# One GpSimd queue, one VectorE queue, one ScalarE queue: moving the side work of an attention pass to other places in its unit

## The chip, the cores and the metric

The kernel runs on one core of one Trainium2 chip. The metric is the device time of one execution in microseconds (us), the median of three runs. Everything is 32-bit float.

## The reference, cut to what matters

The program applies two layers to an input of 8 images, 32 by 32 positions, 512 channels. The first layer is group norm, self-attention with 8 heads and a residual. The second layer, to which the change belongs, is a deformable attention over the first layer's output `x`, read as 4 images:

```python
x_ln = layernorm(x, ln_g, ln_b);  q = x_ln_flat @ wq + bq
o = gelu(depthwise_conv_7x7_stride2(q_img, dw_w) + dw_b)      # 49 taps a channel
offsets = conv_1x1(o, pw_w)                                   # 2 numbers a point
grid = (refs + tanh(offsets) + 1) * ...                       # 16 x 16 points
interp = bilinear(x, grid)                                    # 4 corner rows a point, weighted
k = v = interp @ wv + bv
attn = softmax((q @ mq_w) @ (k @ mk_w).T) per head;  msa = attn @ (v @ mv_w) @ mo_w
z = msa + x
out = gelu(layernorm(z) @ mlp_w + mlp_b) + z
```

In the kernel an "image" is one eighth of the data: 1024 tokens, 256 sampled points.

## The kernel before, in words

The kernel has two passes. The first (lines 396 to 810) does the first layer, and beside it the depthwise convolution of images 0 to 5. The second (from line 813) does the rest of the second layer, and is what the change touches.

**Units.** The second pass is 64 units, `n` = 0 to 63, made by `unit_steps`. A unit is a pair of heads of half an image, so an image has 8 units; the place of a unit in its image, n mod 8, is called its position, p0 to p7, below. A unit consists of scores (TensorE, `sc`), negative row maxima (VectorE, two `nmax` reductions of 128 x 1024 from PSUM), exponentials (ScalarE, `e`: eight activations, each with an accumulator read), two block transposes (VectorE, `sq`), each followed by two DMAs on SyncE's queue that finish the transpose (`sq_d`, `et`), reciprocals of the sums (`rs`), the product with the values one unit later (TensorE, `av`) and its scaling (VectorE, `attH`).

**Back steps.** With each unit one 128-token tile of the half-image before it goes through `back_steps`: `joined` (projection `wo`, then on VectorE `z`, its statistics, and the inverse deviation `mv`, whose power is taken by GpSimd), `norm` (VectorE, `zn`), `turned` (TensorE transposes `zn`, ScalarE copies them to `zT`), and in the next unit `mlp` (`wm`) and `biased` (VectorE, `res`). For every second tile ScalarE applies the GELU to two tiles (`gelu`), which takes one table load ahead of it and one after it to go back to the exponential; GpSimd adds `z` and stores (`end`), and adds a bias row to the next two residual tiles (`add`, `xr`). These last three fall into even units.

**Convolution.** The images 6 and 7 are convolved in the second pass by `conv_steps`, in two lanes. Lane 0 is VectorE alone (one `scalar_tensor_tensor` a tap, tile `chunk`). In lane 1 ScalarE multiplies into one of two `parts` buffers, and GpSimd adds it to `chunk`: a tap therefore waits until the addition two taps before it is done. A lane takes a chunk of 128 channels, 49 taps, after filling its padded plane (`fill` on TensorE, `fill_end` on VectorE).

**Points.** For the images 1 to 7 `point_steps` does, with `b` the image: `conv_load`, `conv_gelu` (ScalarE, the GELU table again), `offsets` (TensorE, then a tanh on ScalarE, then two transposes into a PSUM tile), `targets` (VectorE: `corners`, some twenty tiny instructions that end in the row indices `ii`), and for each half of the points `gather` (four indirect DMAs issued by GpSimd, one a corner, into the four `row` buffers) and `sample` (VectorE, four weighted additions of 128 x 512). The sampled rows are projected to keys and values ahead of the image's first unit (`key_step`, `value_step`).

**Order.** There is no scheduler: `at(place, step)` enters a step under a number, the steps are emitted in the order of these numbers, and `InOrder` keeps each engine's instructions in the order in which they are emitted. The number's whole part is the unit. So the places in the diff are orders in queues, not times. The places around the change, all within unit n:

```python
at(n, scores)                                   # sc, nmax x2, e x8
at(n + 0.02, lambda: att.moved(u, 0))           # first transpose
at(n + 0.04, lambda: att.moved(u, 1))           # second transpose
(n + 0.05, n + 0.13)                            # joined (z ... power on GpSimd), norm (zn)
at(n + 0.06, lambda: query_step(*divmod(n + 1, NHP)))
at(n + 1.1, lambda: att.product(u)); at(n + 1.2, scale)      # of unit n, so 0.1 and 0.2 of the next
ends = (n + 0.6, n + 1.03, n + 1.035)           # turned, mlp, biased
(gelu, 1.72), (end, 2.24)                       # of an odd tile's unit: 0.72 of an odd, 0.24 of an even one
(pair - 1.6, pair - 0.5)                        # fetch, add: `add` at 0.5 of an even unit
```

Of the kernel before, what the change touches and what calls it, by code (L numbers as in the profile page):

```python
# [9 lines left out]
F32 = mybir.dt.float32  # L10
I32 = mybir.dt.int32
AF = mybir.ActivationFunctionType
ALU = mybir.AluOpType
# [4 lines left out]
P = 128  # L18
# [11 lines left out]
NHP = NH // 2  # L30
# [210 lines left out]
def attention_then_deformable_attention(  # L241
# [30 lines left out]
    nc = tc.nc  # L272
# [17 lines left out]
    def mm_tile():  # L290
        return ps_mm.tile([P, QB], F32, tag="mm", name="mm")
# [65 lines left out]
    def at(place, step):  # L357
        due.append((place, len(due), step))
# [37 lines left out]
    with ExitStack() as l0:  # L396
# [3 lines left out]
        nc = InOrder(tc)  # L400
# [366 lines left out]
        for b in range(B):  # L767
# [20 lines left out]
            for hp in range(NHP):  # L788
                for qt in range(NT):
                    n = first + hp * NT + qt  # L790
                    if n % per == 0 and b > 0:
                        last, attT = attT, {}
# [10 lines left out]
                        at=qt % NQT,  # L803
# [9 lines left out]
    with ExitStack() as l1:  # L813
        nc = tc.nc


        def pool(name, bufs=1):
            return l1.enter_context(tc.tile_pool(name=name, bufs=bufs, reuse_waits="tile"))

        first, raw, late, late2, cv, cvhat, wp = (  # L820
            pool(n) for n in ("first", "raw", "late", "late2", "cv", "cvhat", "w2")
        )
        work = pool("work1", 2)
        nc = InOrder(tc)
# [30 lines left out]
        refs = cv.tile([P, 2, 2], F32, tag="refs", name="refs")  # L855
# [58 lines left out]
        chat, room = {}, {}  # L914

        def conv_fetch(b, cb):
            chat[b, cb] = cvhat.tile([P, NT, P], F32, tag="hat", name="hat", bufs=2)
            nc.sync.dma_start(chat[b, cb], hat_d[b][:, :, ts(cb, P)])

        def conv_load(b):  # L920
            room[b, "o"] = cv.tile([P, NC, NS], F32, tag="o", name="o")
            nc.sync.dma_start(room[b, "o"], o_d[b][:, :, :])

        def fill(b, cb, par):
            hat = chat[b, cb]
            room["ps"] = project(lambda c: hat[:, par * NC + c, :], lambda c: wq_r[:, c, :])

        def fill_end(lane, par):
            conv_pad(pads[lane], room["ps"], bq_row, par)
# [10 lines left out]
        def conv_gelu(b):  # L940
            o = room[b, "o"]
            for cb in range(NC):
                nc.scalar.activation(o[:, cb, :], o[:, cb, :], AF.Gelu, bias=dwb[:, cb : cb + 1])

        def offsets(b):
            o = room[b, "o"]
            ps = mm_tile()
            for cb in range(NC):
                nc.tensor.matmul(
                    ps[0:2, 0:NS], lhsT=pww[:, cb, :], rhs=o[:, cb, :],  # L950
                    start=(cb == 0), stop=(cb == NC - 1),
                )
            th = cv.tile([2, NS], F32, tag="th", name="th")
            nc.scalar.activation(th, ps[0:2, 0:NS], AF.Tanh)
            room["th"] = mm_tile()[:, 0:4]
            for h in range(2):
                nc.tensor.transpose(room["th"][:, ts(h, 2)], th[:, ts(h, P)], ident[0:2, 0:2])

        def targets(b):
            room[b, "ii"], room[b, "wt"] = corners(room["th"])  # L960

        def gather(b, h):
            for k in range(4):
                row = room["row", k] = cv.tile([P, C], F32, tag="row", name="row", bufs=4)
                nc.gpsimd.indirect_dma_start(
                    out=row,
                    out_offset=None,
                    in_=mid[b][:, :],
                    in_offset=bass.IndirectOffsetOnAxis(ap=room[b, "ii"][:, k, h : h + 1], axis=0),
                )  # L970
# [14 lines left out]
        def points(b):  # L985
            conv_load(b)
            conv_gelu(b)
            offsets(b)
            targets(b)
            for h in range(2):  # L990
                gather(b, h)
                sample(b, h)

        def corners(th):

            vt = nc.vector

            def small(name, dt=F32):
                return cv.tile([P, 4], dt, tag=name, name=name)

            co = small("co")
            vt.tensor_tensor(co, th, refs.rearrange("p h o -> p (h o)"), ALU.add)
            vt.tensor_scalar(co, co, 1.0, G / 2.0, ALU.add, ALU.mult)
            vt.tensor_scalar(co, co, 1.0, 0.5 * (W - 1), ALU.add, ALU.mult)
            ci = small("ci", I32)
            vt.tensor_copy(ci, co)
            cf = small("cf")
            vt.tensor_copy(cf, ci)
            up = small("up")
            vt.tensor_tensor(up, cf, co, ALU.is_gt)  # L1010
            c2 = cv.tile([P, 2, 4], F32, tag="c2", name="c2")
            vt.tensor_tensor(c2[:, 0, :], cf, up, ALU.subtract)
            vt.tensor_scalar(c2[:, 1, :], c2[:, 0, :], 1.0, None, ALU.add)
            w2 = cv.tile([P, 2, 4], F32, tag="w2", name="w2")
            vt.tensor_tensor(w2[:, 1, :], co, c2[:, 0, :], ALU.subtract)
            vt.tensor_scalar(w2[:, 0, :], w2[:, 1, :], -1.0, 1.0, ALU.mult, ALU.add)
            cl = cv.tile([P, 2, 4], F32, tag="cl", name="cl")
            vt.tensor_scalar(cl, c2, 0.0, float(W - 1), ALU.max, ALU.min)
            inside = cv.tile([P, 2, 4], F32, tag="inside", name="inside")
            vt.tensor_tensor(inside, cl, c2, ALU.is_equal)  # L1020
            vt.tensor_tensor(w2, w2, inside, ALU.mult)
            cl4 = cl.rearrange("p a (h o) -> p a h o", o=2)
            w4 = w2.rearrange("p a (h o) -> p a h o", o=2)
            wt = cv.tile([P, 4, 2], F32, tag="wt", name="wt")
            fi = cv.tile([P, 4, 2], F32, tag="fi", name="fi")
            for k in range(4):
                ax, ay = k % 2, k // 2
                vt.tensor_tensor(wt[:, k, :], w4[:, ax, :, 1], w4[:, ay, :, 0], ALU.mult)
                vt.scalar_tensor_tensor(
                    fi[:, k, :], cl4[:, ay, :, 0], float(W), cl4[:, ax, :, 1], ALU.mult, ALU.add  # L1030
                )
            ii = cv.tile([P, 4, 2], I32, tag="ii", name="ii")
            vt.tensor_copy(ii, fi)
            return ii, wt
# [144 lines left out]
        def conv_steps():  # L1179
            for lane, chunks in enumerate(((0, 3, 6), (1, 2, 4, 5, 7))):  # L1180
                free = 0.5 + lane
                for k in chunks:
                    b, cb = EARLY + k // NC, k % NC
                    first = next(n for n in range(60) if n + 0.49 > free)
                    fills = [first + 0.49, first + 0.55]
                    at(fills[0] - 1.8, lambda b=b, cb=cb: conv_fetch(b, cb))
                    for par, place in enumerate(fills):
                        at(place, lambda b=b, cb=cb, par=par: fill(b, cb, par))
                        at(place + 0.02, lambda lane=lane, par=par: fill_end(lane, par))
                    unit = int(fills[1]) + 1  # L1190
                    i = 0
                    while i < KS * KS:
                        points = unit % (2 * NHP) in range(NHP, NHP + 3)
                        count = 7 if lane else 3 if points else 5
                        for j in range(count):
                            if i == KS * KS:
                                break
                            place = 0.25 + 0.01 * j if not lane else 0.045 + 0.001 * j if j < 4 else 0.65 + 0.01 * j
                            at(unit + place, lambda b=b, cb=cb, i=i, lane=lane: tap(b, cb, i, lane))
                            free = unit + place  # L1200
                            i += 1
                        unit += 1

        def point_steps(b):
            last = 2 * NHP * b - NHP
            at(last - 1.5, lambda: conv_load(b))
            at(last - 0.035, lambda: conv_gelu(b))
            at(last + 0.535, lambda: offsets(b))
            at(last + 0.75, lambda: targets(b))
            for h, (p0, p1) in enumerate(((0.8, 1.22), (1.23, 2.22))):  # L1210
                at(last + p0, lambda h=h: gather(b, h))
                at(last + p1, lambda h=h: sample(b, h))
            first = 2 * NHP * b
            for hp, place in enumerate((-0.82, -0.815, 0.185, 1.18)):
                at(first + place, lambda hp=hp: key_step(b, hp))
            for t, place in enumerate((-0.81, 0.18)):
                at(first + place, lambda t=t: value_step(b, t))
# [75 lines left out]
```

## Time and profile before

| what | value |
|---|---|
| median of 3 runs (lowest, highest) | 3526.83 us (3524.01, 3528.84) |
| the profiled execution: its time, its span | 3522.86 us, 3521.2 us |
| mean granted TensorE clock | 0.984 |
| busy in the span: TensorE, VectorE, ScalarE, GpSimd | 3388.6, 2534.7, 1809.8, 1536.3 us |
| the second pass: first scores, last scores | 2297.0 us, 3451.3 us after the span's start |
| from 2300 us on: TensorE waited for `zn` | 41.7 us in 16 waits |
| one image without a fill of lane 0 (units 16 to 23, 2583.70 to 2740.59) | 156.9 us |

The profiler records one execution. Times are in us from the span's start. Line numbers are of little use here: every recorded call passes through a helper, line 54, so instructions are told apart by their tiles, written out<-in. A timeline line has the start, the duration of a run of equal instructions, the engine, the operation, the count, and in brackets the engine's idle time before it and what ended that.

### The profile page before, as it was taken

To read this page: it belongs to the slowest core of one execution; us is meant where nothing else is said; L and a number is where in the kernel's file an instruction comes from. 1 tells how busy PE (TensorE), PEld (TensorE's weight loads), DVE (VectorE), ACT (ScalarE), POOL (GpSimd) and SP (SyncE) were. 2 spreads that over 40 slices of the span, in tenths; PEclk is the share of its full clock that TensorE was granted. 3 is DMA by queue.
4 is the path that set the end of the run, shared out by engine and by line. 5 is a ranking of instruction groups with operands and counts; after the bars stand their busy time and mean duration, and the time that the engine had idled before them with its cause. 6 is when DMAs were issued, how large, how long until landed. Compare 5 with 4: busy or idle time off the path is not lost.

```text
span 3521.2 us, 45344 instructions
## 1 busy us (share of the span) xinstructions
PE 3388.6 (96%) x14568; PEld 1679.5 (48%) x14568; DVE 2534.7 (72%) x3373; ACT 1809.8 (51%) x3919; POOL 1536.3 (44%) x1903
## 2 busy tenths in 40 slices
PE   7999999999999999999999998889998989899998
PEld 4544554554554554455455444534444444444443
DVE  4767778888888888788888875257777676665654
ACT  3443355566566566566567562245555455554442
POOL 1001226646636646655654653215445353532222
PEclk9999999999999999999999999899999999999999
DMA  4666667766766666767766667445656555565653
GB/s 145 171 159 176 193 170 195 211 160 184 219 164 186 207 169 185 204 174 194 203 174 175 202 177 208 136 157 194 198 175 196 171 181 178 179 199 189 222 184 123
DMA packets 446589, 641.65 MB, mean 182 GB/s; under 512 B 77104, under 2 KB 240944, under 8 KB 444304
## 3 DMA queue, kind: packets, MB, share of 16 engines
q1 hardware_dynamic: 415712, 536.67, 52.4%
q0 software_dynamic: 29488, 100.00, 9.5%
q8 instruction: 116, 1.90, 0.2%
q10 hardware_dynamic: 1152, 2.10, 0.2%
q14 instruction: 121, 0.99, 0.1%
HBM read 246.38 MB, written 123.73 MB: 105 GB/s over the span
## 4 chain that ended last, share of the span: by engine, by line
PE 81%; POOL 4%; ACT 4%; DVE 4%; issue 3%; DMA 2%; SPq 2%; POOLq 0%; ACTq 0%; DVEq 0%
PE mm L54 51%; PE sc L54 16%; PE av L54 15%; ACT e L54 2%; SPq L54 2%; POOL chunk L54 1%; POOL row L54 1%; DVE chunk L54 1%; ACT L54 1%; DVE nmax L54 1%; POOL oa L54 0%; DMA et<-sq_d 0%; DMA sq_d<-sq 0%; POOL rows L54 0%; POOL hat L54 0%
## 5 line engine op out<-in xcount | busy, mean ns | idle before, releaser
L54 ACT ACTIVATE e<-sc,nmax 128x1024 f32<-128x1024 f32 (+1 forms) x1024 | 802.9, 797 | 597.1 <-DVE nmax L54 595.8
L54 DVE TENSOR_REDUCE nmax<-sc 128x1 f32<-128x1024 f32 (+1 forms) x640 | 751.4, 1215 | 383.7 <-PE sc L54 382.7
L54 DVE STREAM_TRANSPOSE sq<-e 128x1024 f32<-128x1024 f32 x640 | 764.3, 1224 | 241.4 <-ACT e L54 218.2
L54 POOL TENSOR_TENSOR oa<-part_x,oa 128x256 f32<-128x256 f32 x852 | 632.2, 742 | 574.7 <-ACT part_x L54 530.3
L54 PE MATMUL sc<-k,q 64*128 64x512 f32 x2048 | 536.6, 619 | 17.1 <-ACT e L54 15.4
L54 ACT ACTIVATE part_x<-pad_x,dww_x 128x256 f32<-128x256 f32 x852 | 434.9, 541 | 222.9 <-POOL oa L54 221.3
L54 PE MATMUL av<-et,v 128*64 128x256 f32 x4096 | 503.5, 388 | 13.9 <-DMA et<-sq 13.0
L54 PE MATMUL mm<-xT,wqkv 128*128 128x512 f32 x1024 | 470.6, 604 | 3.1 <-issue 3.1
L54 PEld LDWEIGHTS av<-et,v 128*64 128x64 f32 x4096 | 275.3, 137 | 319.2 <-issue 161.2
L54 POOL TENSOR_TENSOR chunk<-parts,chunk 128x256 f32<-128x256 f32 x240 | 179.9, 749 | 384.3 <-ACT parts L54 369.2
L54 PEld LDWEIGHTS sc<-k,q 64*128 64x128 f32 x2048 | 186.5, 187 | 280.0 <-issue 190.7
L54 PEld LDWEIGHTS mm<-xT,wqkv 128*128 128x128 f32 x1024 | 187.1, 190 | 240.3 <-issue 234.9
L54 POOL TENSOR_TENSOR mv<-mv,minus_half 128x1 f32<-128x1 f32 x128 | 77.3, 604 | 489.2 <-DVE mv L54 487.1
L54 PEld LDWEIGHTS mm<-wqkv,xT 128*128 128x128 f32 x2048 | 234.1, 192 | 25.7 <-issue 25.7
L54 PE MATMUL mm<-wqkv,xT 128*128 128x128 f32 x2048 | 244.8, 278 | 0.0
L54 PE MATMUL mm<-wm,zT 128*128 128x512 f32 x512 | 238.1, 608 | 1.3 <-ACT zT L54 1.0
L54 PE MATMUL mm<-w,attT 128*128 128x512 f32 x512 | 235.5, 604 | 1.7 <-DVE attT L54 1.7
L54 PE MATMUL mm<-wo,attH 128*128 128x512 f32 x512 | 230.8, 593 | 0.4
L54 PE MATMUL mm<-hat_h,wqq 128*128 128x512 f32 x512 | 230.7, 593 | 0.0
L54 DVE SCALAR_TENSOR_TENSOR od<-pad_x,dww_x,od 128x256 f32<-128x256 f32 x276 | 226.4, 820 | 5.5
L54 ACT ACTIVATION_READ_ACCUMULATOR e<-sc,nmax 128x1 f32 x1024 | 209.2, 204 | 0.0
L54 PE MATMUL mm<-w,hat_x 128*128 128x512 f32 x384 | 172.7, 600 | 0.0
(163 smaller groups left out, 3555.4 us busy)
## 6 DMA issues: line engine op xcount, KB each, us to landing
et<-sq SPq DMA_DIRECT2D x2048, 128.0 KB
sq_d<-sq SPq DMA_DIRECT2D x128, 512.0 KB
et<-sq_d SPq DMA_DIRECT2D x128, 512.0 KB
inv<-rs_d SPq DMA_DIRECT2D x256, 128.0 KB
hat_h<-hat_d SPq DMA_DIRECT2D x16, 1024.0 KB
xr<-mid SPq DMA_DIRECT2D x64, 256.0 KB
x<-in_x_dram POOLq DMA_DIRECT2D x60, 256.0 KB
out_dram<-res POOLq DMA_DIRECT2D x60, 256.0 KB
```

The source lines that it names most:

```text
L54: return self.tc.keep_in_program_order(op(*args, **kwargs))
```

## The change

Four things are moved; no arithmetic changes.

1. Lane 0's taps move from 0.25 of a unit (behind the scaling) to 0.002 (behind the maxima, ahead of the first transpose). They are 6 in a unit rather than 5, and 2 rather than 3 in the units of positions 4 to 6.
2. The first four of lane 1's seven taps in a unit move from 0.045 (ahead of `joined`) to 0.131 (behind `norm`). The other three stay at 0.69 to 0.71.
3. `point_steps` starts one unit earlier: GELU of the convolution at the end of p2, `offsets` at the end of p3. `corners` is split: its first addition, which reads the PSUM tile, is now `shift` at 0.75 of p3; the rest is at 0.011 of p4, behind the maxima and the taps.
4. The first half's `gather` goes from 0.8 of p4 to 0.14 of p4, its `sample` from 0.22 of p5 to 0.012 of p5; the second half's `gather` from 0.23 of p5 to 0.141 of p5, its `sample` from 0.22 of p6 to 0.012 of p6.

```diff
+        def shift(b):
+            co = room[b, "co"] = cv.tile([P, 4], F32, tag="co", name="co")
+            nc.vector.tensor_tensor(co, room["th"], refs.rearrange("p h o -> p (h o)"), ALU.add)
+
         def targets(b):
-            room[b, "ii"], room[b, "wt"] = corners(room["th"])
+            room[b, "ii"], room[b, "wt"] = corners(room[b, "co"])
...
-        def corners(th):
+        def corners(co):
...
-            co = small("co")
-            vt.tensor_tensor(co, th, refs.rearrange("p h o -> p (h o)"), ALU.add)
...
                         points = unit % (2 * NHP) in range(NHP, NHP + 3)
-                        count = 7 if lane else 3 if points else 5
+                        count = 7 if lane else 2 if points else 6
...
-                            place = 0.25 + 0.01 * j if not lane else 0.045 + 0.001 * j if j < 4 else 0.65 + 0.01 * j
+                            place = 0.002 + 0.001 * j if not lane else 0.131 + 0.001 * j if j < 4 else 0.65 + 0.01 * j
...
         def point_steps(b):
-            last = 2 * NHP * b - NHP
+            last = 2 * NHP * b - NHP - 1
             at(last - 1.5, lambda: conv_load(b))
             at(last - 0.035, lambda: conv_gelu(b))
             at(last + 0.535, lambda: offsets(b))
-            at(last + 0.75, lambda: targets(b))
-            for h, (p0, p1) in enumerate(((0.8, 1.22), (1.23, 2.22))):
+            at(last + 0.75, lambda: shift(b))
+            at(last + 1.011, lambda: targets(b))
+            for h, (p0, p1) in enumerate(((1.14, 2.012), (2.141, 3.012))):
                 at(last + p0, lambda h=h: gather(b, h))
                 at(last + p1, lambda h=h: sample(b, h))
```

Because lane 0 goes through its chunks faster, its second and third fills move from units 13 and 25 to units 12 and 24.

## Prediction

> **What bounds the kernel now.** I read the page first, then TensorE's waits from 2300 us on, then the timelines of one image, engine by engine.
>
> ```profile
> PE 3388.6 (96%) x14568; PEld 1679.5 (48%) x14568; DVE 2534.7 (72%) x3373; ACT 1809.8 (51%) x3919; POOL 1536.3 (44%) x1903
> ```
>
> TensorE is the bound; other engines matter only where TensorE waits for them. In the second pass that is one wait:
>
> ```profile
> PE mm L54 <- DVE zn L54: 41.7, 16, 4.9
> ```
>
> TensorE's timeline shows where: p4, p5 and p6 (units 20 to 22 here), the units of the points.
>
> ```profile
> 2675.07 0.65 PE L54 MATMUL mm<-ident,zn 128*128 128x128 f32 x4 [0.86 <-DVE zn L54]
> 2694.89 1.12 PE L54 MATMUL mm<-ident,zn 128*128 128x128 f32 x4 [4.51 <-DVE zn L54]
> 2716.38 0.66 PE L54 MATMUL mm<-ident,zn 128*128 128x128 f32 x4 [3.98 <-DVE zn L54]
> ```
>
> A unit without extra TensorE work takes 14.88 us (unit 19), and reaches the transposes of `zn` at 14.30. What makes `zn` late is a chain: exponentials, transposes, `z`, statistics, GpSimd's power, `zn`. In unit 16 the first transpose starts 8.40 us in, the power ends at 14.44: 6.0 us. With GpSimd free at once (unit 18: 8.38 and 14.14) it is 5.75, which I use. Then `zn` takes 0.55 us, or 1.48 beside a GpSimd addition. The exponentials are late where ScalarE hangs in a lane 1 tap behind GpSimd. GpSimd's timeline of an even unit (p0):
>
> ```profile
> 2597.58 0.56 POOL L54 TENSOR_TENSOR mv<-mv,minus_half 128x1 f32<-128x1 f32 x1
> 2598.09 1.28 POOL L54 TENSOR_TENSOR res<-res,z 128x512 f32<-128x512 f32 x1
> ...
> 2602.41 2.51 POOL L54 TENSOR_TENSOR xr<-xr,bo_row 128x512 f32<-128x512 f32 x2
> 2605.16 2.46 POOL L54 TENSOR_TENSOR chunk<-parts,chunk 128x256 f32<-128x256 f32 x3 [0.24 <-ACT parts L54]
> ```
>
> Two output additions with their stores take 4.32 us (2598.09 to 2602.41), the residual additions 2.75 to the next tap's addition: 7.07 in all. The gathers take 1.25 to 1.3 us each, and ScalarE shows what a tap behind them does (unit 6):
>
> ```profile
> 2377.26 0.95 POOL L54 DMA_INDIRECT row<-mid,ii  x1 [0.30 <-issue]
> 2378.51 0.95 POOL L54 DMA_INDIRECT row<-mid,ii  x1 [0.30 <-issue]
> ...
> 2393.10 0.55 ACT L54 ACTIVATE parts<-pad,dww 128x256 f32<-128x256 f32 x1 [5.37 <-POOL chunk L54]
> ```
>
> VectorE: five taps take 2.56 us alone and 6.87 beside GpSimd's additions; before the transpose it idles 0.86 us in odd units and 4.0 in even ones (ScalarE's GELU and table loads come first).
>
> ```profile
> 2600.17 6.87 DVE L54 SCALAR_TENSOR_TENSOR chunk<-pad,dww,chunk 128x256 f32<-128x256 f32 x5
> 2610.18 1.24 DVE L54 STREAM_TRANSPOSE sq<-e 128x1024 f32<-128x1024 f32 x1 [0.86 <-ACT e L54]
> ...
> 2618.92 2.56 DVE L54 SCALAR_TENSOR_TENSOR chunk<-pad,dww,chunk 128x256 f32<-128x256 f32 x5
> 2629.00 1.24 DVE L54 STREAM_TRANSPOSE sq<-e 128x1024 f32<-128x1024 f32 x1 [4.00 <-ACT e L54]
> ```
>
> **What the Trainium skill says.** "GPSIMD Engine Reference", section 8, Key points: GpSimd shares its SBUF interfaces with VectorE, with contention for two-input instructions and two-port modes; the 2.56 against 6.87 us and the 0.55 against 1.48 agree. "ScalarE: Activation LUTs", What ACT_TABLE_LOAD costs: about 1283 ns a load and some 1380 of drain; the trace has the load at 1283, but the next activation starts 0.01 us behind it, so I add no drain. "TensorE: Matmul & The Clock Gate", Part 1: after an idle window of about 3.4 us the clock is halved; here the transposes behind the 4.51 us wait take 1.12 us rather than 0.60, and those behind 2.47 us are not slowed.
>
> **The change, part by part.** Times run from the unit's first scores; maxima end at 4.38. "Before" is the mean of units 20 to 22, 28 to 30 and 36 to 38.
>
> *Lane 0's taps.* Six take 3.1 us alone, so the slot ends near 7.5; even units have 4.0 idle there: nothing lost. Odd ones: transpose from 5.3 to 7.5. p3 gets TensorE work from `offsets` (below), p5 is bound elsewhere, p7 has key projections until 21.5. p1 transposes `zn` at 16.16; beside GpSimd's late additions its slot may end at 8.8, so 8.8 + 5.75 + 1.5 = 16.1 to 16.4: **+0.2**. The gain, earlier maxima, helps only p5: 9.36 becomes 2.03 there.
>
> *Lane 1's taps behind the norm.* The power no longer waits for them (0.35 us saved), but four additions (3.15 us for four) now stand between it and all that follows on GpSimd: outputs, residuals, gathers, the last three taps. Every `zn` runs beside them: 1.48.
>
> *p3.* The convolution's GELU loses the table switch that it shared with `gelu`: two loads and four activations, 4.2 us, behind `zT`, so exponentials from 4.9, transpose near 7.5, power 13.3, `zn` 14.8. TensorE meanwhile has `offsets`: 1.9 + 0.46 for the tanh + 0.28, transposes at 16.9; length 17.5 for 14.88: **+2.6**.
>
> *p4.* Two taps and the corners (3.7 us from the first scaling to `ii`) put the transpose at 9.2; exponentials (6.2 + 2.05 = 8.25) hide no more than that. Power 14.95, `zn` and transposes 16.5, length 17.1 for 18.4: **-1.3**. A wait of 2.2 us remains.
>
> *p5.* This decides. The GpSimd queue in p4, behind the power: four taps 3.15, four gathers 5.2, outputs and residuals 7.07, and only then the fifth tap's addition, 0.75. ScalarE's seventh tap needs it (0.55 more), and the exponentials of p5, then `q` and the next taps, stand behind that tap on ScalarE; VectorE's transposes wait for them, and TensorE for what follows: 16.7 us after the power. The unit ends 2.1 after its power (1.56 to the transposes, 0.58 for them), so the exponentials start 14.6 us into p5. Before they started at 10.5, held by taps and corners ahead of the maxima. Transpose 14.6 + 2.05 = 16.65, power 22.4, TensorE 23.95, length 24.5 for 20.3: **+4.3**. Maxima, sampling (the last row lands about 2.5 us after its issue, as in the preparation) and `rs` all hide under this.
>
> *p6.* GpSimd in p5: taps 3.15, gathers 5.2, tap 0.75, ScalarE 0.55, less 2.1: 7.55; then table, GELU, table 3.75: exponentials at 11.3. Transpose 13.35, TensorE 20.65, length 21.2 for 21.8: **-0.6**. The old wait, with another owner.
>
> *DMAs.* SyncE's `sq_d` and `et` start up to 3 us later (p5: 4) and need some 9 us; `av` reads them over 12 us into the next unit: hidden. Gather writes and `out_dram` issues count in GpSimd's sums above. Fills move by a unit with the same TensorE work: nothing.
>
> *Sum.* +0.2 + 2.6 - 1.3 + 4.3 - 0.6 = +5.2 for each of images 3 to 5. Image 2 has its fill (7.0 us of TensorE work) in p4 instead of p5: p4 is 21.9 long, so p5's exponentials start at 14.95 + 16.7 - 21.9 = 9.8 and p5 ends at 9.8 + 2.05 + 5.75 + 1.56 + 0.58 = 19.7; p3 to p6 17.5 + 21.9 + 19.7 + 21.2 = 80.3 for 75.4 (units 11 to 14), with p1 +5.1. Images 6 and 7 have no taps: p3 and p4 +0.4, p5 +1.2 (samples beside GpSimd's outputs), p6 -0.3: +1.3 each. Image 1: the score's wait for `q` (2.47) goes, p5 pays as much: 0. Total 15.6 + 5.1 + 2.6 = **+23.3**. On the profiled execution 3522.86 + 23.3 = 3546.2; the median of the runs shown stands 4.0 above it: **3550**.
>
> *Unknown costs.* VectorE's slot beside GpSimd in p1, p5, p7: 0 to 2 us an image. The halved clock after a longer p5 wait: -1 to +2 an image. Gathers at 1.0 rather than 1.3: -1.2 an image. Image 1: -5 to +5. Images 6, 7: 0 to 3.5 each. Own range 3536 to 3571.
>
> **Rivals.** *The waits go* (16 in 100). If the exponentials of p5 and p6 aren't held, the big waits (4.3 and 4.5 an image, four images: 35) and the halved clock behind them (about 1.7 to 3.4 us each, some 15) vanish, less p4's 2.2 an image: about 45 us, **3482**. For it: VectorE's taps and corners leave the path ahead of the maxima, and 0.86 to 4 us of idle time are really there. Against it: the queue sum. It decides if additions behind the gathers reached ScalarE before 7 us into p5, which needs 7.6 us less on GpSimd. *Moved, not removed* (10 in 100). p6's wait shrinks by as much as p5 grows, say because the second gathers run during p5's long wait; the change then ends near **3529**. Against it: the fifth tap still stands behind them. *VectorE beside GpSimd bounds every odd unit* (12 in 100): six taps at 1.37 us (6.87/5) end at 12.6, `zn` 4 us late in p1 and more in p5: 4.5 more in each of four images, **3569**. *Likeliest*: 62 in 100.
>
> **How the numbers follow.** A measurement here can tell about 0.2%, 7 us. Slower by more: 62 + 12 and a part of the third case, 0.77; within: 0.08; faster: 0.15. The range reaches from the third case to above the fourth, 3525 to 3574.
>
> **What would show it.** Right: ScalarE's tap in p5 waiting over 8 us for GpSimd's `chunk`, behind `row`, `res` and `xr`; TensorE's wait for `zn` near 9 us in p5 and 6 in p6; p3 17.5 us long without a wait; maxima at once behind the scores. Wrong: exponentials in p5 under 8 us in, or total waits for `zn` under 20 us.

## The result, and the profile after

| | before | after |
|---|---|---|
| median of 4 runs on one chip (lowest, highest) | 3526.45 us (3524.01, 3528.84) | 3558.47 us (3555.72, 3565.27) |
| ratio of after to before | | 1.0094, interval 1.0076 to 1.0111 |
| profiled execution: time, span | 3522.86, 3521.2 us | 3557.82, 3556.1 us |
| mean granted TensorE clock | 0.984 | 0.979 |
| last scores, after the span's start | 3451.3 us | 3487.5 us |

The kernel became slower, by some 33 us (the ratio's interval is 27 to 39). On the page of after, the busy times:

```profile
PE 3396.6 (96%) x14568; PEld 1685.4 (47%) x14568; DVE 2480.9 (70%) x3373; ACT 1825.8 (51%) x3931; POOL 1531.0 (43%) x1903
```

No engine got more to do, apart from the 12 additional ScalarE instructions (the table loads of p3). VectorE is even 54 us less busy, 37 of them in lane 0's 144 taps of the second pass: 613 ns each on average instead of 871. TensorE is 8 us busier with the same 14568 matmuls, so some of them took longer. Most of the loss is in the waits of TensorE from 2300 us on (engine and tile that waited, what it waited for, then the sum, the number and the longest wait, us):

```profile
PE mm L54 <- DVE zn L54: 67.1, 18, 9.4
```

It was 41.7 in 16, and 4.9 the longest. From its first scores to its last the second pass grew by 33.9 us: TensorE waited 26.4 us longer in all, and its matmuls there took 7.5 us longer. TensorE's timeline of units 20 to 22 (p4, p5, p6) shows where they are now:

```profile
2691.55 0.66 PE L54 MATMUL mm<-ident,zn 128*128 128x128 f32 x4 [0.77 <-DVE zn L54]
...
2715.62 1.11 PE L54 MATMUL mm<-ident,zn 128*128 128x128 f32 x4 [9.13 <-DVE zn L54]
2716.66 3.79 PE L54 MATMUL sc<-keys,q 64*128 64x256 f32 x16
...
2736.76 0.66 PE L54 MATMUL mm<-ident,zn 128*128 128x128 f32 x4 [3.84 <-DVE zn L54]
```

p4's wait is as short as it was (0.86 before), p5's has doubled from 4.51, p6's is where it was (3.98 before). Behind p5's wait the next unit's scores take 3.79 us rather than 2.00, about half the pace; below this is called half clock. p4 is shorter because `offsets` went to p3. Who makes `zn` late in p5 (unit 21, from 2692.13)? First VectorE's timeline of after:

```profile
2694.16 2.35 DVE L54 TENSOR_REDUCE nmax<-sc 128x4 f32<-128x1024 f32 x2 [2.07 <-PE sc L54]
...
2708.83 1.25 DVE L54 STREAM_TRANSPOSE sq<-e 128x1024 f32<-128x1024 f32 x1 [1.85 <-ACT e L54]
```

The maxima come at once behind the scores, 2.03 us in, as the change places them. The transpose comes 16.70 us in, and it waited for ScalarE. So ScalarE's timeline is next:

```profile
2706.45 0.53 ACT L54 ACTIVATE parts<-pad,dww 128x256 f32<-128x256 f32 x1 [12.18 <-POOL chunk L54]
2706.89 0.45 ACT L54 ACTIVATE e<-sc,nmax 128x256 f32<-128x256 f32 x1
```

Two taps fit into the two buffers; the third, the seventh of its unit, stood for 12.18 us until GpSimd had added the one two before it, and the exponentials stood behind it in ScalarE's queue with their maxima long there. And what GpSimd did meanwhile:

```profile
2689.97 0.55 POOL L54 TENSOR_TENSOR mv<-mv,minus_half 128x1 f32<-128x1 f32 x1 [9.89 <-DVE mv L54]
2690.49 3.20 POOL L54 TENSOR_TENSOR chunk<-parts,chunk 128x256 f32<-128x256 f32 x4
2693.85 1.04 POOL L54 DMA_INDIRECT row<-mid,ii  x1 [0.17 <-issue]
...
2697.72 1.12 POOL L54 DMA_INDIRECT row<-mid,ii  x1 [0.30 <-issue]
2698.87 1.28 POOL L54 TENSOR_TENSOR res<-res,z 128x512 f32<-128x512 f32 x1
...
2703.25 2.49 POOL L54 TENSOR_TENSOR xr<-xr,bo_row 128x512 f32<-128x512 f32 x2
2705.70 2.67 POOL L54 TENSOR_TENSOR chunk<-parts,chunk 128x256 f32<-128x256 f32 x3
```

It idled 9.89 us ahead of the power, the stretch in which the four additions lay before, and then did everything in a row: four additions, four gathers, two outputs, two residual tiles, and only then the fifth tap.

The lengths of the units of one image, from scores to scores, in us (units 19 to 23, and 16 to 23 together), of all the kernels in this text. As in the prediction, "image 3" means these units, 16 to 23, in which the points of image 3 are made; "image 1" is units 0 to 7, "image 7" units 48 to 55.

| | p3 | p4 | p5 | p6 | p7 | units 16 to 23 |
|---|---|---|---|---|---|---|
| before | 14.88 | 18.37 | 20.27 | 21.03 | 23.63 | 156.89 |
| after | 17.44 | 15.71 | 24.53 | 20.69 | 23.62 | 160.70 |
| e1, outputs later | 17.44 | 15.71 | 24.13 | 21.20 | 23.16 | 160.36 |
| e2, taps ahead of the norm | 17.44 | 15.69 | 22.45 | 19.35 | 21.98 | 155.62 |
| e3, points as before | 14.88 | 19.35 | 20.25 | 22.16 | 23.01 | 158.36 |
| e4, seven taps in front | 17.44 | 15.72 | 24.83 | 21.79 | 23.04 | 161.53 |
| e5, lane 0 alone | 14.88 | 18.17 | 19.34 | 20.85 | 21.98 | 153.93 |
| e6, gathers in odd units | 14.88 | 16.57 | 16.54 | 16.59 | 21.99 | 148.04 |
| e7, e6 and residuals in odd units | 14.88 | 17.35 | 14.88 | 17.35 | 23.63 | 149.56 |
| e8, e7 and five taps in front | 14.88 | 16.36 | 14.88 | 16.38 | 21.98 | 145.95 |

In e6, e7 and e8, whose points start a unit earlier than after's, p2 takes up what p3 gives.

### The profile page after: what moved, and what is told of

The parts are those of the page before. It is cut to its first block, busy times and chain, and to the rows that moved or that the text cites. A ratio compares the mean times of both kernels' runs of the same rounds, so it can differ in the third digit from the quotient of the medians.

```text
span 3556.1 us, 45315 instructions
## 1 busy us (share of the span) xinstructions
PE 3396.6 (96%) x14568; PEld 1685.4 (47%) x14568; DVE 2480.9 (70%) x3373; ACT 1825.8 (51%) x3931; POOL 1531.0 (43%) x1903
## 4 chain that ended last, share of the span: by engine, by line
PE 74%; issue 11%; POOL 5%; DMA 4%; DVE 3%; ACT 2%; SPq 1%; POOLq 0%; ACTq 0%; DVEq 0%
PE mm L54 46%; PE sc L54 14%; PE av L54 13%; SPq L54 1%; POOL chunk L54 1%; ACT e L54 1%; POOL row L54 1%; DMA sq_d<-sq 1%; POOL xr L54 1%; DMA inv<-rs_d 1%; DMA row<-mid,ii 1%; DVE sq L54 1%; DVE nmax L54 1%; DMA et<-sq 1%; POOL oa L54 0%
## 5 line engine op out<-in xcount | busy, mean ns | idle before, releaser
L54 ACT ACTIVATE parts<-pad,dww 128x256 f32<-128x256 f32 x240 | 124.5, 546 | 198.7 <-POOL chunk L54 198.1
```

Of the source, the lines that this page charges most:

```text
L54: return self.tc.keep_in_program_order(op(*args, **kwargs))
```

## The experiments

Every kernel was timed together with the kernel before (3523.9 us beside e1 to e4, 3523.5 beside e5 to e8); the ratios are to that. The edits shown are cut to the expressions that change. The question of the first five: is the loss the GpSimd queue that ScalarE's tap stands behind, and which of the moves puts it there? The queue theory says that what is taken out of that stretch of GpSimd's queue, or put behind the tap, comes back in p5. The rival says that VectorE's work beside GpSimd is what delays `zn`.

**e1: the two outputs behind the fifth tap.** Only the place of `end` changes, from 0.24 to 0.75 of an even unit.

```diff
-  (end, 0.28 if tail else 0.74 if over else 2.24),
+  (end, 0.28 if tail else 0.74 if over else 2.75 if n < 60 else 2.24),
```

> The changed kernel with the two output additions and their stores moved from 0.24 of an even unit to 0.75, behind lane 1's last three taps (units below 60). Queue theory (p5's exponentials stand behind a ScalarE tap whose buffer is freed only behind everything on GpSimd): 4.3 us leave the queue ahead of the fifth addition of p4, p5's first transpose moves from 16.7 to about 12.6 and p5 from 24.5 to about 20.4 in three images and by about 2.5 in image 2: about 15 us less, near 3543. p6 stays near 21.5, because p5 has no outputs. VectorE theory (the taps, corners and samplings that now stand ahead of the transposes make them late): no change, 3558, and p5 stays near 24.5.

Measured: 3548.58 us, ratio 1.0064 (1.0040 to 1.0089). p5 shortened by 0.4 us only in image 3, and by 1.4 and 2.0 in images 4 and 5. In ScalarE's timeline of e1 the tap's wait fell from 12.18 us by the outputs' share:

```profile
2695.73 0.53 ACT L54 ACTIVATE parts<-pad,dww 128x256 f32<-128x256 f32 x1 [8.12 <-POOL chunk L54]
```

The transpose followed, 12.65 us in rather than 16.70. But VectorE's timeline of e1 has a wait behind it that wasn't there:

```profile
2698.11 1.25 DVE L54 STREAM_TRANSPOSE sq<-e 128x1024 f32<-128x1024 f32 x1
...
2702.96 0.69 DVE L54 TENSOR_TENSOR res<-mm,bm_row 128x512 f32<-128x512 f32 x1 [3.61 <-DMA out_dram<-res]
```

`res` has three buffers. Stored later, they come free later, and `biased`, ahead of the next `z` on VectorE, waits 3.61 us for the store. So the queue theory holds for the exponentials (4 us out of the queue, 4 us earlier), and in image 3 the time went into a new wait. In images 4 and 5 that wait is 1.1 us; there the sampling ends last, and the transpose starts 13.9 to 14.0 us in. Where the wait does not arise, in p5 of image 2, the unit is 17.45 us long, for 19.15 in after.

**e2: lane 1's first four taps back ahead of the norm.** All else as in after.

```diff
-  0.131 + 0.001 * j if j < 4
+  0.045 + 0.001 * j if j < 4
```

> The changed kernel with lane 1's first four taps back at 0.045, ahead of joined. Queue theory: four additions (3.15 us) leave the stretch between the power and the fifth tap, and the gathers start 3 us earlier as well; p5 about 21.4 and p6 about 18.5 rather than 24.5 and 21.3, about 23 us less in the four images, near 3535. The power waits some 0.3 us longer in each unit, which shows only in p4. VectorE theory: nothing gained, and the later power makes it 1 to 3 us slower, near 3560.

Measured: 3530.75 us, ratio 1.0012 (1.0003 to 1.0021), as expected within 5 us: of the 33 us, 29 are gone. The tap's wait in p5 fell from 12.18 us to 10.63. TensorE's timeline of e2, in p5 and p6:

```profile
2703.29 1.11 PE L54 MATMUL mm<-ident,zn 128*128 128x128 f32 x4 [7.04 <-DVE zn L54]
...
2723.10 0.65 PE L54 MATMUL mm<-ident,zn 128*128 128x128 f32 x4 [2.07 <-DVE zn L54]
```

The additions fill GpSimd's idle time ahead of the power again. The waits of p5 and p6 are 2.1 and 1.8 us shorter than in after, less than the 3.2 us of the four additions; in p6 the exponentials start 2.8 us earlier, and the sampling then ends last. The gathers are still in the queue behind the power, and p5 still waits 7 us.

**e3: the points as before.** The lanes as in after; GELU, `offsets`, corners, gathers and samplings in their old places.

```diff
-  last = 2 * NHP * b - NHP - 1
+  last = 2 * NHP * b - NHP
-  at(last + 1.011, lambda: targets(b))
-  ((1.14, 2.012), (2.141, 3.012))
+  at(last + 0.751, lambda: targets(b))
+  ((0.8, 1.22), (1.23, 2.22))
```

> The changed kernel with the points where they were (offsets in p4, corners ahead of the maxima of p5, first gather at 0.8 of p4, second at 0.23 of p5, samplings behind the scaling), and the taps of both lanes in their new places. Queue theory: the gathers no longer stand between the power and the fifth addition in p4, so p5 is about 19.5 and p6 about 21; p3 is 14.9 again and p4 17.5; images 6 and 7 as before the change. About 3516, that is 10 us under the kernel before and 42 under the changed one. VectorE theory: the taps ahead of the transposes cost in every odd unit, and the kernel stays above 3535.

Measured: 3538.45 us, ratio 1.0036 (1.0028 to 1.0044). Missed by 22 us: I had expected it faster than before. p3 came back to 14.88, but p4 grew to 19.35 and p5 stayed at 20.25. TensorE's and VectorE's timelines of e3 (unit 21 starts at 2688.91) tell why:

```profile
2688.11 0.28 PE L54 MATMUL mm<-ident,th 2*128 2x2 f32 x2 [2.37 <-ACT th L54]
```

```profile
2692.77 3.56 DVE L54 TENSOR_SCALAR w<-w 128x4 f32<-128x4 f32 x1
...
2698.54 2.35 DVE L54 TENSOR_REDUCE nmax<-sc 128x4 f32<-128x1024 f32 x2
```

ScalarE's tanh now stood behind the taps behind the norm, and TensorE waited for it. And with the corners ahead of the maxima, beside the outputs and residuals that GpSimd does for p4, one instruction of 128x4 elements took 3.56 us and the maxima came 9.63 us in. What the GpSimd stretch costs was thus only handed from ScalarE's tap to VectorE's corners. The time is above the 3535 us that the rival theory had set, but not by its mechanism: p1 and p3, odd units with six taps ahead of the transposes, are as long as before (16.74 and 14.88).

**e4: all seven taps in front of the gathers.** In p4 and p5 lane 1's last three taps stand with the first four, so no tap is behind gathers and outputs.

```diff
-  if j < 4
+  if j < (7 if unit % (2 * NHP) in (NHP, NHP + 1) else 4)
```

> The changed kernel with all seven taps of lane 1 behind the norm, ahead of the gathers, in p4 and p5. No ScalarE tap is then behind a gather, and p5's exponentials start at once, near 3.3 us in. Queue theory, with what the trace of the changed kernel shows of the rows (the last one lands 5 us and more behind its issue): the gathers end 9 us into p5, and the sampling, which stands ahead of the transposes, ends near 14.8; p5 about 22.2 rather than 24.5, p6 about 22.2 rather than 21.3: some 5 us less, near 3553, with VectorE waiting for the rows instead of for the exponentials. If the rows don't matter, p5 falls to about 16 and the kernel to about 3525.

Measured: 3559.91 us, ratio 1.0085 (1.0063 to 1.0108): the same as after. ScalarE's and VectorE's timelines of e4, in p5 (unit 21 starts at 2700.07):

```profile
2703.42 0.48 ACT L54 ACTIVATE e<-sc,nmax 128x256 f32<-128x256 f32 x1
```

```profile
2709.38 1.23 DVE L54 TENSOR_SCALAR smp<-row,wt 128x512 f32<-128x512 f32 x1 [4.01 <-DMA row<-mid,ii]
2711.54 5.72 DVE L54 SCALAR_TENSOR_TENSOR smp<-row,wt,smp 128x512 f32<-128x512 f32 x3 [0.93 <-DMA row<-mid,ii]
2717.18 1.24 DVE L54 STREAM_TRANSPOSE sq<-e 128x1024 f32<-128x1024 f32 x1
```

The exponentials are free, 3.35 us in. But the sampling, which stands ahead of the transpose, waits 4 us for the gathered rows, goes on beside GpSimd's outputs and residuals (three additions in 5.72 us rather than 2.33), and the transpose is at 17.1 us all the same. So a second chain, by way of the rows, lies under the first. e4 itself made it longer, by three additions ahead of the gathers. In after the sampling does hide under the tap, as predicted, with 0.7 to 3.0 us to spare in images 3 to 5.

**e5: before, with lane 0's move alone.**

```diff
-  count = 7 if lane else 3 if points else 5
-  place = 0.25 + 0.01 * j if not lane
+  count = 7 if lane else 2 if points else 6
+  place = 0.002 + 0.001 * j if not lane
```

> The kernel before the change with lane 0's taps alone in their new places and counts (six or two, behind the maxima). Queue theory: this part gains. p5 no longer has three slow taps ahead of its maxima, its first transpose starts near 8.3 instead of 12.6, p5 takes about 15.5 instead of 20.3; p6 stays near 21.8, since its exponentials stand behind the second gathers: about 17 us less than before, near 3507. The other two parts then cost: the taps behind the norm about 31 (from here to the run with the points as before), the points about 24. VectorE theory: the taps ahead of the transposes are what costs, and this kernel is slower than 3524.

Measured: 3520.91 us, ratio 0.9989 (0.9977 to 1.0000): at most a few microseconds of gain, and not the 17 that I expected. VectorE's timeline of e5 in p5 (unit 21 starts at 2681.55):

```profile
2683.29 3.60 DVE L54 CAST cf<-ci 128x4 f32<-128x4 int32 x1
...
2689.99 2.35 DVE L54 TENSOR_REDUCE nmax<-sc 128x4 f32<-128x1024 f32 x2
```

The maxima are still 8.44 us in (9.36 before), held by the corners beside GpSimd's outputs and residuals; p5 is 0.9 us shorter.

**What the five say together.** Call the three moves L (lane 0's taps), T (lane 1's taps behind the norm) and P (the points). The ratios: L 0.9989 (e5), L and P 1.0012 (e2), L and T 1.0036 (e3), all three 1.0094. So on top of L, T costs 17 us without P and 29 with it; P costs 8 without T and 20 with it. Together they cost 12 us more than one by one; with the intervals of the four ratios that is 4 to 21, so the sign is shown and the size is not. T and P without L weren't run. It fits what the timelines show: both push work into the one stretch of GpSimd's queue between the power of an even unit and the fifth tap.

**e6: the gathers in odd units.** If that is so, the remedy is not to reorder the stretch but to thin it. e6 is after with the taps as in e2 and the points two units ahead of before's places: corners in p3, gathers behind the last taps of p3 and p5 (an odd unit has no outputs and no residuals), each with more than a unit to land; samplings in p5 and p7.

```diff
-  points = unit % (2 * NHP) in range(NHP, NHP + 3)
-  count = 7 if lane else 2 if points else 6
+  points = unit % (2 * NHP) in (3, 5, 7)
+  count = 7 if lane else (1 if unit % (2 * NHP) == 3 else 2) if points else 6
-  0.131 + 0.001 * j if j < 4
+  0.045 + 0.001 * j if j < 4
-  last = 2 * NHP * b - NHP - 1
+  last = 2 * NHP * b - NHP - 2
-  ((1.14, 2.012), (2.141, 3.012))
+  ((1.72, 3.012), (3.72, 5.012))
```

> A version built from what the runs show: the changed kernel with lane 1's first four taps ahead of joined again, and the points two units earlier than before instead of one: offsets at the end of p2, corners behind the maxima of p3 (one tap of lane 0 there), the gathers behind lane 1's last taps in the odd units p3 and p5, which have no outputs on GpSimd, and the samplings behind the maxima of p5 and p7, each over a unit behind its gather. Queue theory: no ScalarE tap stands behind a gather any more and no sampling waits for rows: p3 15.0, p4 15.7, p5 16 to 17, p6 15.7, p2 2.6 longer for the offsets; 10 us less than before in each of three images and 8 in image 2: near 3486. If VectorE's work ahead of the transposes is what costs, it stays above 3515.

Measured: 3493.66 us, ratio 0.9904 (0.9887 to 0.9920). The waits of TensorE in e6, from 2300 us:

```profile
PE mm L54 <- DVE zn L54: 19.7, 13, 2.6
```

That is far under the 3515 us above which the rival theory had it. p4, p5 and p6 are some 16.6 us each. How much of the gain is the thinner queue alone is not shown: the kernel before with only its points moved to odd units wasn't run, so nothing says what the moves of VectorE's work add.

**e7: the residuals in odd units too.** e6, with the back step's fetch and `add` moved so that GpSimd's residual additions fall behind an odd unit's taps.

```diff
-  places = (pair - 1.6, pair - 0.5), (n + 0.05, n + 0.13), ends
+  places = (pair - 2.6, pair - 1.285), (n + 0.05, n + 0.13), ends
```

> The same with the residual additions in odd units, behind lane 1's last taps and ahead of the gathers (their fetch a unit earlier). 2.75 us leave the queue ahead of the fifth addition of p4, p5 starts its exponentials near 4.5 instead of 7, and its samplings meet less of GpSimd: p5 15.0 to 15.5, 1 to 2 us less an image, near 3480. If p5 is by then bound elsewhere: no change from the run before it.

Measured: 3505.93 us, ratio 0.9931 (0.9905 to 0.9956): 12 us slower than e6, where I had expected it to be faster. p5 has the full 14.88, but p4 and p6 grew by 0.8. There GpSimd does the residual additions, the four gathers and the unit's own first four taps in one row, and the power stands right behind them, as its timeline of e7 shows in p4:

```profile
2670.55 2.68 POOL L54 TENSOR_TENSOR xr<-xr,bo_row 128x512 f32<-128x512 f32 x2
...
2678.44 3.15 POOL L54 TENSOR_TENSOR chunk<-parts,chunk 128x256 f32<-128x256 f32 x4
2681.55 0.56 POOL L54 TENSOR_TENSOR mv<-mv,minus_half 128x1 f32<-128x1 f32 x1
```

`zn` waits 1.64 us for this power, 0.97 in e6. But TensorE's waits for `zn` are as long in sum as in e6 (20.3 and 19.7 us). What grew is the time of its matmuls, by 9.2 us in the second pass, and that is all of the 9.0 us by which the pass is longer. In p4 and p6 of images 2 to 5 its waits went from 1.5 to 1.7 us in e6, none of them followed by half clock, to 2.0 to 2.8 us, six of eight followed by it. One of e7's four executions took 3494 us with a mean granted clock of 0.987, like e6's four (3493 to 3494, 0.986 to 0.988); the other three took 3505 to 3508 with 0.983 or 0.984. TensorE's timeline of e7, two of these waits:

```profile
2683.69 0.66 PE L54 MATMUL mm<-ident,zn 128*128 128x128 f32 x4 [2.40 <-DVE zn L54]
...
2840.11 1.12 PE L54 MATMUL mm<-ident,zn 128*128 128x128 f32 x4 [2.39 <-DVE zn L54]
2841.16 3.09 PE L54 MATMUL sc<-keys,q 64*128 64x256 f32 x16
```

The first is followed by transposes of 0.66 us, the second, as long, by transposes of 1.12 and scores of 3.09.

**e8: five taps in front, two behind, in odd units.** e7, with one tap of an odd unit taken out of the crowded end.

```diff
-  if j < 4 else
+  if j < 4 + unit % 2 else
```

> The same with lane 1's seven taps divided 5 and 2 instead of 4 and 3 in odd units. The two late taps find both buffers free, so that ScalarE starts the GELU of the even unit without waiting for GpSimd: the even units' exponentials start about 1.3 us earlier and p4 and p6 lose their last wait of 0.8 us each: 1.6 us less an image, near 3474. If the even units' VectorE slot is already the later one: no change.

Measured: 3480.57 us, ratio 0.9866 (0.9849 to 0.9882). By the ratios it is some 47 us under before and 80 under after, and 7 us above what I had expected. The waits of TensorE in e8:

```profile
PE mm L54 <- DVE zn L54: 12.2, 9, 1.8
```

The exponentials of p4 and p6 start 1.0 us earlier than in e7, and their waits fell from 2.4 to 1.4 us. All waits for `zn` are now under 1.98 us, and none is followed by half clock: of the 20 us by which the second pass is shorter than e7's, 12.3 are matmuls that took less time. The sampling's additions run at full speed (2.33 us for three). What is still open, VectorE's timeline of e8 shows: `zn` at 1.48 us beside GpSimd's output, and a power half a microsecond late in p4 and p6:

```profile
2672.14 1.48 DVE L54 TENSOR_SCALAR zn<-z,mv 128x512 f32<-128x512 f32 x1 [1.13 <-POOL mv L54]
```

## Why the prediction was right, and where it was off

**The mechanism held.** The step that "decides", p5's exponentials behind a tap behind four additions, four gathers, two outputs and two residuals, is in the trace as it was added up: transpose 16.65 us in predicted, 16.70 measured; power's end 22.4 and 22.45; length 24.5 and 24.53; TensorE's wait "near 9", 9.13; the tap's wait "over 8", 12.18. That it agrees to 0.1 us is in part luck: the queue took 16.4 us, not 16.7, and p4 ended 1.6 us behind its power, not 2.1, and these two nearly cancel. e1 shows the cause of the late exponentials by itself: 4 us out of that queue, transpose 4 us earlier in image 3.

**p3** was 17.44 us without a wait for 17.5 predicted. **p1** was 16.74 for 16.9: "VectorE beside GpSimd bounds every odd unit" falls there, where six taps fit. But VectorE's work beside GpSimd is not nothing: in e3 and e5 the corners, and in e4 the rows and the sampling, decide p5 where ScalarE's tap doesn't.

**p4** ended sooner, 15.71 for 17.1. The corners take 3.0 us ahead of the transpose where GpSimd is idle, not 3.7, and `zn` 0.94 beside the taps' 256-wide additions, not 1.48, which is its time beside the 512-wide output. **p6**: the wait was 3.84 us and not 6, though the unit was about as long as predicted (20.7 to 22.3 for 21.2): after p5's 9 us wait TensorE's scores took 1.8 us longer, and `zn` took 0.94 us here too, so that less of the unit was left to wait in.

**The sum was too small**: +23.3 predicted, about +33 measured. By image, predicted and measured in the profiled executions: image 1, 0 and +8.4; image 2, +5.1 and +5.8; images 3 to 5, +15.6 and +12.4; images 6 and 7, +2.6 and +7.2. So the terms that were mis-sized are these:

- *Image 1 was put at zero.* Three things were there. In p0 eight matmuls of `wo` (the tiles mm<-wo,rep_w) took 6.68 us, at half clock, behind the same 3.45 us wait behind which they had taken 3.70 before. I don't put these 3 us down to the change: the wait is the same to 0.02 us in every kernel here, the eight matmuls took 5.2 to 6.5 us in the profiles of all eight experiments, e5 and e8 among them, and only before's profile has 3.70. In p6 the sampling waited for its rows, the term below: p6 grew by 3.8 us, and p7, whose scores came at half clock behind p6's wait, by 2.2. And the DMAs of the transposes, which the prediction had hidden, aren't here: `av` waits 2.3 us for `et` in p5 and 0.5 in p6, where it didn't wait before.

- *"The last row lands about 2.5 us after its issue, as in the preparation"* is the step that failed. In the pass the last row is usable 5.0 us after its issue's end in p5 of image 3, and 6.5 in p6 of image 1. By the trace's landing times the last of four gathers landed 4.5 to 7.5 us after its issue in all 14 cases in the pass of after, and 2.6 in both of the preparation. GpSimd's, VectorE's and TensorE's timelines of after, in p6 of image 1:

```profile
2396.45 0.94 POOL L54 DMA_INDIRECT row<-mid,ii  x1 [0.30 <-issue]
```

```profile
2403.89 0.75 DVE L54 SCALAR_TENSOR_TENSOR smp<-row,wt,smp 128x512 f32<-128x512 f32 x1 [2.12 <-DMA row<-mid,ii]
```

```profile
2411.24 1.11 PE L54 MATMUL mm<-ident,zn 128*128 128x128 f32 x4 [4.34 <-DVE zn L54]
```

The sampling thus ended 3.9 us after the exponentials were far enough for the transpose; in image 1 no longer wait covers that. I had taken the figure from a quieter stretch: the DMA engines were busy 36% of the time there, and 91% in p5 of image 3. That this is the reason wasn't tested.

- *Images 6 and 7* were given 1.2 us for p5, "samples beside GpSimd's outputs". p5 was 18.06 us for 16.8: three additions took 5.51 us there (2.33 undisturbed), with a wait for the rows ahead of them, in VectorE's timeline of after:

```profile
3182.73 5.51 DVE L54 SCALAR_TENSOR_TENSOR smp<-row,wt,smp 128x512 f32<-128x512 f32 x3 [0.93 <-DMA row<-mid,ii]
```

Behind the 3.1 us wait in p5 of image 6 the next scores took 3.67 us rather than 2.00, and p6 grew by 2.0 where -0.3 was predicted. The profiled execution also began its second pass 2.3 us later, in the preparation that the change doesn't touch.

**The rivals**: "the waits go" needed 7.6 us less on GpSimd in that stretch; e6 and e8, which take the gathers (5.0 us) and then the residuals (2.5) out of it, do about that. Its terms (35 and 15, less 2.2 in each of four images) sum to 41 us, not 45, so to 3486 rather than 3482. e8's 3481 is near, but in part by luck: it gains 11 to 12 us in images 3 to 5, and 5 in image 2, where the sum took all four alike. "Moved, not removed" needed p6's wait to shrink as p5's grew; it shrank by 0.1 in image 3.

**Left open.** Which of the waits between 2 and 3.5 us are followed by half clock and which not, no run here settles. What the moves of VectorE's work are worth in e6 to e8, apart from the thinner queue, wasn't measured. The gap between e8's units of 16.4 and 14.88 is read from its trace; closing it wasn't tried.

## What to carry to other kernels

When work is moved behind something on one engine's in-order queue, add up everything that then stands between that point and the next instruction on which a different engine waits; the idle time ahead of the move is lost, and what filled it is now in the way. When one wait is taken away, work out the second chain under it before counting the gain: here an output's buffer (e1), the gathered rows (e4) and the corners (e3) each stood within a few microseconds of the tap. A crowded stretch is mended by moving a part of it to a unit where the engine has less to do, and then looking at what it crowds there (e6, e7, e8). And look at how long the waits are, not only at their sum: e7 waits as long as e6 in all, and loses 9 us because its waits are fewer and longer.

## What the runs showed of the hardware that I had not expected

- One VectorE instruction beside GpSimd's two-input additions can be held for some 3 us, whatever its size: one of 128x4 elements, 0.17 us alone, took 3.56 and 3.60 us (e3, e5), and 128x512 additions, 0.75 us alone, took up to 3.72 (after) and 4.03 (e2). In the cases at 3.56 and 3.60 us, and in the slowest of e4's sampling additions (3.36), GpSimd's two residual additions, back to back, lay inside. Most of the other tiny instructions in the same stretch stayed at 0.15 to 0.17 us.
- Rows gathered by an indirect DMA landed 2.6 us after the last of four issues in the preparation, and 4.5 to 7.5 us after it in the pass (after).
- In the second pass of the ten profiles together, no wait of TensorE under 1.98 us is itself followed by half clock, 31 of the 46 waits from 1.99 to 3.46 us are, and all 72 from 3.49 us on. The wait of 2.47 us in image 1, at full pace behind it in before, has half clock behind it in e6 and e7. Each of the 101 stretches of slowed matmuls has a wait of 1.98 us or more among the 24 matmuls up to it. Over the 24 matmuls behind such a wait the slowed pace cost 1.7 to 5.6 us, 3.6 in the median.
